# Per-feature sums of K taken from the diagonals of a row of sums, by VectorE in three separate steps

## The chip, the cores and the metric

The kernel runs on one core of a Trainium2 chip, as one launch. The metric is the device time of that launch in microseconds (us). Before the change the median of three runs is 722.59 us, the lowest 722.54 us and the highest 722.98 us. The profile is of one further execution, which took 722.83 us.

A core has five engines that run their own instruction lists and wait for each other by semaphores: TensorE (PE in the profile; its weight loads are shown apart as PEld), VectorE (DVE), ScalarE (ACT), GpSimd (POOL) and SyncE (SP), which issues the DMAs. Matrix products land in PSUM, eight banks of 128 partitions by 2 KB; all else lies in SBUF.

## The reference, cut to what matters

The layer is a residual of two branches on a layer-normalised input of 2 batches x 1024 tokens x 512 features: linear attention with 16 heads of 32 features, and a feed-forward part with low-rank experts. The change touches only the attention's sums of K.

```python
Q = jax.nn.elu(Q) + 1.0
K = jax.nn.elu(K) + 1.0
KV = jnp.einsum('bhsd,bhse->bhde', K, V)
QKV = jnp.einsum('bhsd,bhde->bhse', Q, KV)
K_sum = jnp.sum(K, axis=-2)                      # one number per batch, head and feature
QK_sum = jnp.einsum('bhsd,bhd->bhs', Q, K_sum)
out = QKV / (QK_sum[..., None] + 1e-08)
```

`K_sum` is needed twice: as the stationary operand of the product that makes the denominators `QK_sum`, and, times the bias of V, as a part of `KV`.

## The kernel before, in words

All engines but SyncE follow the order in which the program is written (a manual schedule). The sixteen tiles of 128 tokens are handled in eight pairs, `m` = 0 to 7, by `k_pair` (L421). Pairs 0 to 3 are batch 0 and pairs 4 to 7 batch 1. A pair computes K for its two tiles by seven quarter-size products (a Strassen scheme; banks `ua`, `x`, `lo`), applies elu, transposes the next tiles (bank `pt`), and multiplies the finished K tiles of the pair before by the normalised x, accumulating in the four banks `pg0` to `pg3` (`accumulate`, L410). GpSimd adds up K itself in `ksum`, 128 partitions x 512 features (`add_keys`, L412). Summing `ksum` over its partitions gives `K_sum`.

Within `k_pair` there are named places, "n", "a" and "b", where a table `hooks` (L688) hangs further work. Place "a" is behind the product 6 and its addition (L470), ahead of the transposes of the next tile; place "b" is behind the additions of L480 and L481 and ahead of the token sums of the next pair (L399 to L403). Whatever is hung there stands in every engine's list at that point.

The class `Finish` ends a batch's attention sums. `copies` moves the four `pg` banks to SBUF by ScalarE. `sums` makes `pr`, the product of a 128x128 block of ones with `ksum`: every partition of `pr` holds the whole row of 512 sums. VectorE then multiplies it by the bias of V into `ksr` (L541). `chunk_sums` makes `pc`: four products, one for each block of 128 features, with that block of `ksum` as the stationary operand and one column of ones as the moving one (L527), which puts the sums along the partitions, one column per block. VectorE copies them by four instructions into `ksd` (L531) and GpSimd shifts a second copy of it (L534). `ksd` is not read before the product `pd` of the denominators (L879, at 169 us). `values` makes `pv` and adds `ksr` to it in `kvd` (L557); `outputs` multiplies `kvd` by the output weights into the four `pko` (L562), which ScalarE copies (L563).

For batch 0 these steps hang in pairs 4 to 7: `sums` and `chunk_sums` together in pair 5, place "a". For batch 1 they hang in the first query unit (`query_unit`, L759; places named "P6", "P5" and so on after the product that they follow), which computes Q by seven products and elu with the work split over TensorE, ScalarE and VectorE.

PSUM banks are given by `Finish.bank` (L511). For batch 0 `pr0` takes bank `pt`, and `pc0` bank `x`. For batch 1 each new tile takes the next of `pg0` to `pg3` in turn, so that a tile waits for the readers of the one four places before it. After the first query unit the eight banks are handed to a new pool, whose first tiles are the five `psa` (L569), then `pxa` (L857) and `pd`.

Of the kernel before, what the change touches and what calls it, by code (L numbers as in the profile page):

```python
# [10 lines left out]
F32 = mybir.dt.float32  # L11
AF = mybir.ActivationFunctionType
ALU = mybir.AluOpType
AX = mybir.AxisListType

P = 128
# [21 lines left out]
def layer_kernel(  # L38
# [23 lines left out]
    nc = tc.nc  # L62
# [13 lines left out]
    DK = D // N_HEADS  # L76
    HPC = P // DK
    NC = D // P
# [23 lines left out]
    def pool(stack, name, bufs=1, **k):  # L102
        return stack.enter_context(tc.tile_pool(name=name, bufs=bufs, reuse_waits="tile", **k))
# [28 lines left out]
    p2w = pool(p2_stack, "p2w", bufs=2)  # L132
# [3 lines left out]
    p1 = pool(p1_stack, "p1", side="right")  # L136
    p1w = pool(p1_stack, "p1w", bufs=2, side="right")

    ident = const.tile([P, P], F32, name="ident")
# [40 lines left out]
    bv_sb = p1.tile([P, NC], F32, name="bv_sb")  # L180
# [11 lines left out]
    ones = p1.tile([P, P], F32, name="ones")  # L192
# [50 lines left out]
    def bank(name, shape=None, tag=None):  # L243
        tag = tag or (next(tags) if tags else "ps")
        return ps_pool[0].tile(shape or [P, TB], F32, tag=tag, name=name)


    warm = bank("warm", [P, NC, P], "pt")

    def warm_up(n):  # L250
# [3 lines left out]
    warm_up(WARM[0])  # L254

    pbk = bank("pbk", tag="x")
    nc.tensor.matmul(pbk, ones, bk_sb, start=True, stop=True)
    warm_up(WARM[1])
# [52 lines left out]
    def transpose_x(n, tag="pt"):  # L311
        i = TILES[n]
        pt = [bank(f"pt{i}", [P, NC, P], tag)] * 2
        if n == 0:
            pt[1] = bank("pt0_1", [P, NC, P], "ua")
        for c in range(NC):
            nc.tensor.transpose(pt[c // 2][:, c, :], xns[n][:, ts(c, P)], ident)
        for k in range(2):
            nc.scalar.copy(xnT[i // TPBATCH][k][:, :, ts(i % TPBATCH, P)], pt[k][:, 2 * k : 2 * k + 2, :])
# [101 lines left out]
    def k_pair(m, late, hooks={}):  # L421
# [69 lines left out]
        sums = pair_token_steps(2) if m == 1 else iter(())  # L491
        ea = elu_min(ka, f"ek{na}")
        next(sums, None)
        nc.vector.tensor_add(kb[:, HI], ua[:, 0:HD], bk_sb[:, HI])
        nc.vector.tensor_copy(lb, ua[:, HD:])
        elu_k(ka, ea)
        list(sums)
        eb = elu_min(kb, f"ek{nb}")
        if more:
# [4 lines left out]
    class Finish:  # L504
# [5 lines left out]

        def bank(self, name, shape=None):  # L511
            if self.b == 0:
                return bank(name, shape, "pt" if name in ("pr0", "pko0_3") else "x")

            self.made += 1
            return ps_kv_pool.tile(shape or [P, TB], F32, tag=f"pg{(self.made - 1) % NC}", name=name)

        def copies(self):
            self.gt = slot(7, [NC, D], f"gt{self.b}")
            for m in range(NC):  # L520
                nc.scalar.copy(self.gt[:, m, :], self.pg[m])

        def chunk_sums(self):

            pc = self.bank(f"pc{self.b}", [P, NC])
            for c in range(NC):
                nc.tensor.matmul(pc[:, c : c + 1], self.ksum[:, ts(c, P)], ones[:, 0:1], start=True, stop=True)  # L527
            k = ksd[self.b]
            for h in range(HPC):
                rows = slice(h * DK, (h + 1) * DK)  # L530
                nc.vector.tensor_copy(  # L531
                    k[rows, 0, :, 8 * h : 8 * h + 4], pc[rows, :].unsqueeze(2).to_broadcast([DK, NC, 4])
                )
            nc.gpsimd.tensor_copy(k[:, 1, :, 4:32], k[:, 0, :, 0:28])  # L534

        def sums(self):

            pr = self.bank(f"pr{self.b}")
            nc.tensor.matmul(pr, ones, self.ksum, start=True, stop=True)
            self.ksr = p1.tile([P, NC, P], F32, tag="ksr", name=f"ksr{self.b}")  # L540
            nc.vector.tensor_mul(  # L541
                self.ksr, bv_sb.unsqueeze(2).to_broadcast([P, NC, P]), pr.rearrange("p (c n) -> p c n", n=P)
            )

        def values(self):

# [29 lines left out]
    def route(n):  # L576

        sc = p2.tile([P, TPB, E], F32, tag="sc", name=f"sc{n}")
        nc.scalar.activation(sc, lg[n], AF.Sigmoid)
        bi = p2.tile([P, TPB, E], F32, tag="bi", name=f"bi{n}")  # L580
        nc.vector.tensor_add(bi, sc, eb_sb.unsqueeze(1).to_broadcast([P, TPB, E]))

        sh = [P, TPB, E, E]
        bj = bi.unsqueeze(2).to_broadcast(sh)
        be = bi.unsqueeze(3).to_broadcast(sh)
        gt = p2w.tile(sh, F32, tag="tmp", name=f"gt{n}", bufs=3)
        nc.vector.tensor_tensor(gt, bj, be, ALU.is_gt)
        eq = p2.tile(sh, F32, tag="eq", name=f"eq{n}")
        nc.vector.tensor_tensor(eq, bj, be, ALU.is_equal)
        nc.vector.tensor_mul(eq, eq, before.unsqueeze(1).to_broadcast(sh))  # L590
        nc.vector.tensor_add(gt, gt, eq)
        rank = bi
        nc.vector.tensor_reduce(rank, gt, AX.X, ALU.add)
        ws = wts[n // 2][:, n % 2]
        nc.vector.scalar_tensor_tensor(ws, rank, TOP_K - 0.5, sc, ALU.is_lt, ALU.mult)
        sm = p2.tile([P, TPB], F32, tag="sm", name=f"sm{n}")
        nc.vector.tensor_reduce(sm, ws, AX.X, ALU.add)
        nc.vector.tensor_scalar_add(sm, sm, DIV_EPS)
        nc.vector.reciprocal(sm, sm)
        nc.vector.tensor_scalar_mul(sm, sm, SCALE)  # L600
        nc.vector.tensor_mul(ws, ws, sm.unsqueeze(2).to_broadcast([P, TPB, E]))

    def weights_across(b):

        rows = 2 * TPB * E
        pw = fin[1].bank(f"pw{b}")
        nc.tensor.transpose(pw[0:rows, 0:P], wts[b].rearrange("p n t e -> p (n t e)"), ident)
        wx = p2.tile([rows, P], F32, tag="wx", name=f"wx{b}")
        nc.scalar.copy(wx, pw[0:rows, 0:P])
        nc.sync.dma_start(out=w_dram[b].rearrange("e t p -> t e p"), in_=wx)  # L610
        for i in range(2):
            for e in range(E):
                k = i * ER + e * RANK
                nc.sync.dma_start(
                    out=wT[b][k : k + RANK, :],
                    in_=w_dram[b][e].rearrange("t p -> (t p)").partition_broadcast(RANK),
                )
# [58 lines left out]
    for n in range(2):  # L676
# [9 lines left out]
    fin = []  # L686
# [8 lines left out]
        (6, "n"): [lambda: next(wq_sums)],  # L695
        (7, "n"): [lambda: pair_token_sums(0)],
        (4, "b"): [lambda: fin.append(Finish(0, pg, ksum)), lambda: fin[0].copies()],
        (5, "a"): [lambda: fin[0].sums(), lambda: fin[0].chunk_sums()],
        (6, "a"): [lambda: fin[0].values()],
        (6, "b"): [lambda: fin[0].outputs((0,))],  # L700
        (7, "a"): [lambda: route(0), lambda: fin[0].outputs((1,))],
        (7, "b"): [lambda: fin[0].outputs((2, 3))],
    }
# [281 lines left out]
    def last_sums():  # L985
# [7 lines left out]

    query_unit(0, {
        "P2": [last_sums],
        "P6": [lambda: fin[1].chunk_sums(), lambda: fin[1].sums(), lambda: route(3)],
        "P5": [lambda: fin[1].values(), lambda: weights_across(0)],
        "P7": [lambda: next(sums1), lambda: next(sums1), lambda: weights_across(1)],
        "P3": [lambda: fin[1].outputs((0, 1, 2, 3))],
# [532 lines left out]
    def next_pair(j):  # L1532

        pf = {}


        def pe(i):
            return lambda: pf.update({i: fold_pe(j, FREE[i], (i,))})

        def adds(i):  # L1540
            return lambda: fold_adds(j, i, pf.pop(i))

        def sums(eng, *ps):
            return lambda: list(inner_weight_sums(eng, j, ps))

        last = {}

        def last_sums(n):
            def f():
                g = last.setdefault(0, inner_weight_sums(nc.vector, j, (1, 5, 6)))  # L1550
                for _ in range(n):
                    next(g, None)

            return f

        return (
            {"6c": [pe(0)], "1d": [adds(0)], "6d": [pe(1)], "7": [adds(1)]},
            {"6c": [lambda: fold_sums(j, 0)], "2c": [lambda: fold_sums(j, 1), sums(nc.gpsimd, 3)],
             "3b": [sums(nc.gpsimd, 2), last_sums(2)], "3d": [last_sums(3)]},
        )  # L1560
# [617 lines left out]
```

## Time and profile before

| | |
|---|---|
| median of 3 runs (lowest, highest) | 722.59 us (722.54, 722.98) |
| the profiled execution | 722.83 us |
| its span, first to last instruction | 721.0 us |
| busy: PE, DVE, ACT, POOL | 714.4, 578.4, 198.3, 142.6 us |
| granted TensorE clock | 1.000 |
| 76 to 88 us: PE, DVE, ACT busy | 12.00, 9.40, 4.72 of 12 us |
| 136 to 148 us: PE, DVE, ACT busy | 12.00, 6.10, 8.23 of 12 us |
| 160 to 172 us: PE, DVE, ACT busy | 12.00, 7.60, 7.45 of 12 us |

The span is what the engines' records cover; the 1.83 us between it and the execution's time lie around it. The rows by stretch are the ones in which the changed instructions stand: pair 5 runs from about 76 to 93 us, the first query unit from about 125 to 169 us. A product of two fp32 operands appears as two passes, each with its own weight load, so that the four small products of one `pc` are eight weight loads and eight matmuls in the records. In a timeline line the first number is the start, the second the length of the merged group, and a bracket tells how long the engine had been idle and what ended that. In the chain of waits the numbers are start and length of each piece, counted from the end of what released it.

### The profile page before, as it was taken

Reading aid. Unit: us, or ns where it says so; the run is one execution under the profiler, and the core shown is the slowest. Engines: PE = TensorE matmul, PEld = TensorE weight load, DVE = VectorE, ACT = ScalarE, POOL = GpSimd, SP = SyncE. Lnnn points to the kernel's source line nnn. Section 1 sums busy time; section 2 is a strip of 40 time slices with the busy share of each in tenths; the row PEclk is TensorE's granted clock in tenths of the full one; section 3 lists DMA queues with packets and bytes.
Section 4 is the critical chain, followed back from the end, with each engine's and each line's share of the span. In section 5 each row is a group of like instructions: output and inputs, shape, how many; then the busy total and the mean of one; then the engine's idle time right before and its main releaser. Section 6 shows DMA issues by size and latency. Waiting matters only on the chain.

```text
span 721.0 us, 9901 instructions
## 1 busy us (share of the span) xinstructions
PE 714.4 (99%) x3426; PEld 491.4 (68%) x3426; DVE 578.4 (80%) x1327; ACT 198.3 (28%) x438; POOL 142.6 (20%) x176
## 2 busy tenths in 40 slices
PE   8999999999999999999999999999999999999998
PEld 6666676454434566566566566566688899899897
DVE  7788767777688678778778778878988889998884
ACT  3534413453532333333333333333200000000000
POOL 4033011101001752211211311544520100000000
PEclk9999999999999999999999999999999999999999
DMA  5243001214475101211211201334662444433101
GB/s 174 103 129 112 1 0 42 57 34 134 128 204 171 30 27 35 89 48 44 89 38 51 87 32 58 117 127 136 205 193 107 128 156 126 146 120 110 59 16 45
DMA packets 61734, 66.85 MB, mean 93 GB/s; under 512 B 10866, under 2 KB 49522, under 8 KB 61428
## 3 DMA queue, kind: packets, MB, share of 16 engines
q1 hardware_dynamic: 61154, 66.20, 29.9%
q8 instruction: 27, 0.44, 0.3%
q14 instruction: 23, 0.19, 0.1%
q10 hardware_dynamic: 530, 0.02, 0.0%
HBM read 44.11 MB, written 22.09 MB: 92 GB/s over the span
## 4 chain that ended last, share of the span: by engine, by line
PE 85%; DVE 12%; ACT 2%; issue 1%; POOL 0%; DVEq 0%; POOLq 0%
PE ab L1205 16%; PE b L1265 8%; PE po L1953 7%; PE pg L410 5%; PE pqu L778 4%; PE pya L1782 4%; PE pxa L1782 4%; PE pyb L1782 3%; PE ph L1650 3%; PE x L1205 3%; PE pxb L1782 2%; PE pyc L1782 2%; PE pxa L857 2%; PE b L1260 2%; PE pqv L778 2%; PE pr L1092 2%
## 5 line engine op out<-in xcount | busy, mean ns | idle before, releaser
L1265 PE MATMUL b<-t,w 128*128 128x512 f32 x160 | 83.2, 601 | 0.1
L410 PE MATMUL pg<-kt,xn 128*128 128x512 f32 x128 | 58.7, 594 | 0.5 <-DVE kt L354 0.5
L1287 POOL TENSOR_TENSOR r<-r,r 128x512 f32<-128x512 f32 x20 | 30.1, 1524 | 85.2 <-DVE t L1287 83.0
L1205 PE MATMUL ab<-ti,wi 128*128 128x256 f32 x180 | 45.4, 379 | 0.0
L1205 PEld LDWEIGHTS ab<-ti,w 128*128 128x128 f32 x140 | 25.1, 189 | 29.5 <-DVE r L1233 8.2
L1287 DVE TENSOR_TENSOR r<-r,r 128x512 f32<-128x512 f32 x60 | 43.2, 762 | 0.0
L1205 PEld LDWEIGHTS ab<-ti,wi 128*128 128x128 f32 x180 | 34.2, 190 | 13.2 <-issue 4.8
L1205 PE MATMUL ab<-ti,w 128*128 128x256 f32 x140 | 41.2, 387 | 0.5 <-DVE r L1233 0.2
L410 PEld LDWEIGHTS pg<-kt,xn 128*128 128x128 f32 x128 | 23.1, 190 | 22.6 <-issue 20.6
L1233 DVE TENSOR_TENSOR r<-r,ab 128x256 f32<-128x256 f32 x50 | 20.9, 419 | 21.6 <-ACT r L1230 21.1
L1238 ACT COPY r<-ab 128x256 f32<-128x256 f32 x50 | 18.6, 373 | 71.1 <-PE ab L1205 71.1
L1265 PEld LDWEIGHTS b<-t,w 128*128 128x128 f32 x160 | 29.2, 190 | 10.6 <-issue 5.9
L1241 DVE TENSOR_TENSOR r<-r,ab 128x256 f32<-128x256 f32 x50 | 20.9, 419 | 16.2 <-ACT r L1238 15.9
L1215 ACT COPY r<-ab 128x256 f32<-128x256 f32 x50 | 18.7, 374 | 48.4 <-PE ab L1205 47.1
L1953 PE MATMUL po<-wd,f 128*128 128x256 f32 x140 | 30.9, 380 | 0.1
L419 POOL TENSOR_TENSOR ksum<-ksum,kt 128x512 f32<-128x512 f32 x12 | 15.8, 1318 | 71.4 <-DVE lg L456 42.4
L1226 ACT COPY r<-ab 128x256 f32<-128x256 f32 x50 | 18.6, 373 | 40.7 <-PE ab L1205 40.7
L1896 DVE TENSOR_TENSOR f<-f 128x256 f32<-128x256 f32 x84 | 29.4, 423 | 0.1
L1953 PEld LDWEIGHTS po<-wd,f 128*128 128x128 f32 x140 | 26.4, 190 | 4.4 <-issue 0.9
L1205 PE MATMUL ab<-xnT,w 128*128 128x256 f32 x100 | 29.4, 390 | 0.0
L1205 PE MATMUL ab<-xnT,wi 128*128 128x256 f32 x100 | 28.1, 379 | 0.0
L1205 PEld LDWEIGHTS ab<-xnT,w 128*128 128x128 f32 x100 | 18.1, 189 | 10.9 <-issue 4.5
(483 smaller groups left out, 1652.1 us busy)
## 6 DMA issues: line engine op xcount, KB each, us to landing
h_dram<-h SPq DMA_DIRECT2D x40, 256.0 KB
f<-h_dram SPq DMA_DIRECT2D x10, 512.0 KB
x_ring<-in_x_dram SPq DMA_DIRECT2D x16, 256.0 KB
q_dram<-qt SPq DMA_DIRECT2D x16, 256.0 KB
xr<-in_x_dram SPq DMA_DIRECT2D x16, 256.0 KB
out_dram<-xr SPq DMA_DIRECT2D x15, 256.0 KB
w<-in_w_gate_dram SPq DMA_DIRECT2D x10, 256.0 KB
w<-in_w_up_dram SPq DMA_DIRECT2D x10, 256.0 KB
```

The costliest lines, as they stand in the source:

```text
L410: nc.tensor.matmul(pg[m], xns[n][:, ts(m, P)], kt, start=(j == 0), stop=(j == TPBATCH - 1))
L778: nc.tensor.matmul(banks[c], wqs[p][:, k, ts(c, P)], tsum[b][p][:, k, :], start=(start and k == 0), stop=(k == 1), skip_group_check=True,)
L1205: nc.tensor.matmul(out, w, t, start=start, stop=True, skip_group_check=True)
L1215: nc.scalar.copy(self.r[0][:, H0], self.ua)
L1233: nc.vector.tensor_add(self.r[1][:, H1], self.r[1][:, H1], self.lo)
L1241: nc.vector.tensor_add(self.r[1][:, H0], self.r[1][:, H0], self.lo)
L1265: nc.tensor.matmul(pb[m], ws[m][:, A_OF[p], ts(k, P)], tsum[b][p][:, k, :], start=start, stop=True, skip_group_check=True)
L1287: eng.tensor_add(to[m], t[m], v[m])
L1650: nc.tensor.matmul(phs[u][g * ER : (g + 1) * ER, :], a, f[:, g, :], start=(ns[0] == 0 and n == 0), stop=(last and n == len(chunks) - 1), s ...
L1782: nc.tensor.matmul(o, lhsT, rhs, start=first, stop=True, skip_group_check=True)
L1896: op(t[:, at, :], t[:, x_, :], t[:, y, :])
L1953: nc.tensor.matmul(ps[p][:, q, :], lhsT, rhs, start=start, stop=stop, skip_group_check=True)
```

## The change

The sums along the partitions are no longer made by TensorE. `pr` holds the row of all sums in every partition, so the sum of feature 128c + p stands in partition p at column p of block c, on the diagonal of each block. VectorE multiplies `pr` by the identity, broadcast over the four blocks (`diag`), and adds up each block along its row (`kc`). The four copies into `ksd` then read `kc` in SBUF where they read `pc` in PSUM.

The work is cut in three functions. `sums` issues only the product `pr`. `read_sums` issues the two VectorE instructions that read `pr`. `chunk_sums` issues the reduction, the four copies and the GpSimd copy. For batch 0 they stand in pair 5 "a", pair 5 "b" and pair 6 "b"; for batch 1 all three stand where both stood, in "P6", now with `sums` first. `pr0` takes bank `x`; with one tile fewer, the later tiles of batch 1 each move on by one bank.

```diff
         def bank(self, name, shape=None):
             if self.b == 0:
-                return bank(name, shape, "pt" if name in ("pr0", "pko0_3") else "x")
+                return bank(name, shape, "pt" if name == "pko0_3" else "x")
...
+        def sums(self):
+
+            self.pr = self.bank(f"pr{self.b}", [P, NC, P])
+            nc.tensor.matmul(self.pr, ones, self.ksum, start=True, stop=True)
+
+        def read_sums(self):
+            self.ksr = p1.tile([P, NC, P], F32, tag="ksr", name=f"ksr{self.b}")
+            nc.vector.tensor_mul(self.ksr, bv_sb.unsqueeze(2).to_broadcast([P, NC, P]), self.pr)
+
+            sh = [P, NC, P]
+            self.diag = p2w.tile(sh, F32, tag="tmp", name=f"diag{self.b}", bufs=3)
+            nc.vector.tensor_mul(self.diag, ident.unsqueeze(1).to_broadcast(sh), self.pr)
+
         def chunk_sums(self):
-
-            pc = self.bank(f"pc{self.b}", [P, NC])
-            for c in range(NC):
-                nc.tensor.matmul(pc[:, c : c + 1], self.ksum[:, ts(c, P)], ones[:, 0:1], start=True, stop=True)
+            kc = p1w.tile([P, NC], F32, tag="kc", name=f"kc{self.b}")
+            nc.vector.tensor_reduce(kc, self.diag, AX.X, ALU.add)
             k = ksd[self.b]
             for h in range(HPC):
                 rows = slice(h * DK, (h + 1) * DK)
                 nc.vector.tensor_copy(
-                    k[rows, 0, :, 8 * h : 8 * h + 4], pc[rows, :].unsqueeze(2).to_broadcast([DK, NC, 4])
+                    k[rows, 0, :, 8 * h : 8 * h + 4], kc[rows, :].unsqueeze(2).to_broadcast([DK, NC, 4])
                 )
             nc.gpsimd.tensor_copy(k[:, 1, :, 4:32], k[:, 0, :, 0:28])
-
-        def sums(self):
-
-            pr = self.bank(f"pr{self.b}")
-            nc.tensor.matmul(pr, ones, self.ksum, start=True, stop=True)
-            self.ksr = p1.tile([P, NC, P], F32, tag="ksr", name=f"ksr{self.b}")
-            nc.vector.tensor_mul(
-                self.ksr, bv_sb.unsqueeze(2).to_broadcast([P, NC, P]), pr.rearrange("p (c n) -> p c n", n=P)
-            )
...
-        (5, "a"): [lambda: fin[0].sums(), lambda: fin[0].chunk_sums()],
+        (5, "a"): [lambda: fin[0].sums()],
+        (5, "b"): [lambda: fin[0].read_sums()],
         (6, "a"): [lambda: fin[0].values()],
-        (6, "b"): [lambda: fin[0].outputs((0,))],
+        (6, "b"): [lambda: fin[0].outputs((0,)), lambda: fin[0].chunk_sums()],
...
-        "P6": [lambda: fin[1].chunk_sums(), lambda: fin[1].sums(), lambda: route(3)],
+        "P6": [lambda: fin[1].sums(), lambda: fin[1].read_sums(), lambda: fin[1].chunk_sums(), lambda: route(3)],
```

## The prediction, on record before the changed kernel ran

> **What bounds the kernel.** I read the page first: busy shares, then the engines' shares of the chain of waits.
>
> ```profile
> PE 714.4 (99%) x3426; PEld 491.4 (68%) x3426; DVE 578.4 (80%) x1327; ACT 198.3 (28%) x438; POOL 142.6 (20%) x176
> ...
> PE 85%; DVE 12%; ACT 2%; issue 1%; POOL 0%; DVEq 0%; POOLq 0%
> ```
>
> TensorE is the bound on the whole, and no DMA stands on the chain. But TensorE's busy time is modelled, so I next read the chain of waits from 60 to 180 us, where the touched instructions are.
>
> ```profile
> 82.08 0.86 PE pr L539 x2
> 82.94 0.79 PE pc L527 x8
> 83.72 0.65 PE pt L317 x4
> ...
> 141.97 0.79 PE pc L527 x8
> 142.76 0.97 PE pr L539 x2
> 143.73 3.43 PE pqu L778 x8
> ```
>
> The products that the change removes are on the chain both times. Until 75.67 the chain there is VectorE's; from then to 250 us it is TensorE's without a break. So TensorE time removed in pair 5 or in the first query unit counts, as far as the other engines can follow. That is the question, and the timeline answers it at each place.
>
> **What is removed.** Sixteen passes of one column. In the timeline `pc` starts at 82.77 and the transposes `pt` at 83.72: 0.95 us for eight. Those transposes also wait in the program for `ksr`'s read of bank `pt`, which ends at 82.97 + 0.69 = 83.66; with `pr0` in bank `x` that wait goes too, so they start at 82.77. In the query unit `pc` starts at 141.81, `pr` at 142.62, the next product at 143.56. With `pr` at 141.81 and its usual two passes of 0.43, that product starts at 142.67: 0.89 us. Together **1.84 us** of TensorE.
>
> Here a rule speaks against the change. The Trainium skill (TensorE: Matmul & The Clock Gate, "Back-to-back issue gap") gives a matmul of 1 to 64 columns a floor of about 25 ns; sixteen would be worth 0.40 us, as an estimate from that page, and the work given to VectorE in exchange would look dear. The row says 0.86 us for the last seven weight loads and their passes, over 0.1 us each: each pass is paced by its 128-column weight load. I take the row.
>
> **What is added on VectorE**, per batch: `diag`, the same form as L541 (0.69); the reduction of 128x512, between L593 (128x256, 0.42) and the 0.69 of a 128x512 operation, so 0.69. The four copies stay at 0.72: they read SBUF now, and small SBUF operations (L275, 0.17) cost what these did in PSUM (0.17). So 1.38 us per batch is new, and for batch 0 everything is also moved: `ksr` with `diag` (1.42 with gaps) to pair 5 "b", the reduction with the copies (1.45) to pair 6 "b". No step issues a DMA, and SP's queue is not passed. On POOL the copy of L534 (0.28) goes behind the memset of `kvd` for batch 0 and delays it by 2.3 us for batch 1, where `kvd` is wanted at 152.62: nothing. POOL's first `ksum` addition of batch 1 is released by `pr` in place of `pc`, some 0.8 us sooner: nothing.
>
> **Pair 5, batch 0.** The cover is this:
>
> ```profile
> 87.48 0.42 DVE L481 TENSOR_TENSOR kt<-kt,klo 128x256 f32<-128x256 f32 x1
> ...
> 88.72 0.43 DVE L399 TENSOR_TENSOR t<-xnT,xnT 128x256 f32<-128x256 f32 x1 [0.82 <-ACT xnT L319]
> ...
> 90.32 0.41 DVE L490 TENSOR_TENSOR kt<-kt,klo 128x256 f32<-128x256 f32 x1
> ...
> 91.90 0.69 DVE L354 SCALAR_TENSOR_TENSOR kt<-kt,ek 128x512 f32<-128x512 f32 x1 [0.29 <-ACT ek L350]
> ...
> 93.15 0.41 PEld L410 LDWEIGHTS pg<-kt,xn 128*128 128x128 f32 x2
> ```
>
> L399 waits 0.82 us for ScalarE's copy of the transposed tile. That copy stands behind a chain from the statistics (L263 to L275), which VectorE begins at 82.57 and no longer at 84.51, since `ksr` and the copies are gone from "a". Its square root is then held only by its table load: from the end of the other tile's copy, 84.12, come 1.28 (load), 0.20, 1.28 (load), 0.20 and 0.65 for the copy, so with gaps the tile is there at 87.82 (88.70 before). VectorE: L480 follows TensorE, now at 86.07; L481 ends at 86.95; `ksr` and `diag` end at 88.41; L399 starts at 88.45. So VectorE is 0.27 us earlier than before, and TensorE 0.95. Behind L399 VectorE has no idle time down to L354, so that difference of 0.68 us runs into TensorE's waits, which had these margins: product 7 of pair 6 waits for L490 (ended 90.73, load at 91.40); product 1 for L495 (91.61, 92.27); the accumulation for L354 (92.59, 93.15). All were 0.56 to 0.67. The last falls short by 0.12, and by some 0.15 with the semaphore; part may hide in the usual lead of a load over its pass. I charge **0.15**. If the statistics did not come earlier, the charge would be about 0.9. Bank `x` is a new wait: product 2 of pair 6 (its load at 89.56 after the shift, the whole TensorE list behind it) waits for `diag`, which ends at 88.41. That is covered by 1.1 us. First gain: 0.80.
>
> In pair 6 the reduction and copies go between L481 (ends 104.56 after a shift of 0.80) and L399, whose data were there at 105.6. L403 then ends at about 107.8, L490 comes 0.25 late against the shifted TensorE, and the product behind it has 0.9 us to spare (L490 ended 108.78, load at 109.72). Nothing. In pair 7 L490 again stood idle 2.77 us for TensorE: the lag is gone there.
>
> **The first query unit, batch 1.** VectorE's added 1.38 us fall before this wait, in which L581 had been idle 3.40 us since `ksr`:
>
> ```profile
> 147.59 0.23 ACT L579 ACTIVATE sc<-lg 128x32 f32<-128x32 f32 x1
> ...
> 147.85 0.19 DVE L581 TENSOR_TENSOR bi<-sc,eb_sb 128x32 f32<-128x32 f32 x1 [3.40 <-ACT sc L579]
> ...
> 159.24 0.24 ACT L609 COPY wx<-pw 64x128 f32<-64x128 f32 x1
> ...
> 159.81 0.19 PEld L562 LDWEIGHTS pko<-wo_sb,kvd 128*128 128x128 f32 x1 [0.24 <-issue]
> ...
> 164.72 0.69 DVE L837 TENSOR_TENSOR qt<-qt,pqv 128x512 f32<-128x512 f32 x1 [0.35 <-PE pqv L778]
> ```
>
> So they are hidden. But the same wait shows that ScalarE and VectorE do not move with TensorE here. ScalarE's list from the last copy of product 6 (142.01) to the sigmoid at 147.59 depends on nothing that the change advances; from 147.85 VectorE works through without idling to 155.9, then both alternate to ScalarE's copies of `pko` (162.95 to 165.00). All this stays in place while TensorE runs 0.89 us ahead, until it needs them (times here without the 0.80 of pair 5, which shifts all alike):
> - `pko3` takes the bank of `pw1` and waits for L609, which ends at 159.48. Its load stood at 159.81, would stand at 158.92, and goes at 159.54; its pass then starts 0.19 later at 159.73, against 160.23 before. 0.50 is left.
> - `psa0` now inherits the bank of `pko1`, not `pko0`: it waits for the second L563 copy, 162.95 + 2 x 0.513 = 163.98, and starts at about 164.23 against 164.52: 0.29 left.
> - `psa4` waits for the second L837, which waited 0.35 for TensorE; it can come forward only to the end of the first, 163.69 + 0.68 plus a gap: 0.31 left.
>
> From there L787, the elu and `pd` (which had about 0.3 to spare behind the last L790) follow with the same 0.31. Second gain: **0.30** of 0.89.
>
> The skill's Trace Analysis page (Perfetto Trace Analysis, "Identifying the Most-Contended Engine") would name the engine of highest occupancy and have it relieved first; by that all 1.84 us count, and TensorE is indeed busy 12.00 of 12 us from 160 to 172. The three waits above say 1.10. I go by the waits.
>
> **Sum.** 0.80 + 0.30 = 1.10 us. Later the chain alternates between TensorE and VectorE with no DMA on it, so I let the gain pass whole to the end. The profiled execution, 722.83 us (721.0 span, 1.83 around it), gives 721.7; it stands 0.24 above the median of the runs, from which the same gain gives 721.5. I say **721.6 us**.
>
> **The rivals.**
> 1. *Both gains in full* (721.0, 24%). For it: both `pc` groups are on the chain, and the margins at `pko3` and `psa` are near 0.3, of the size of my reading errors in lead times. Against it: three separate waits would have to be softer than they look.
> 2. *VectorE is short in pair 5* (722.3, 14%). The statistics do not come earlier, or `diag` and its neighbour cost more: TensorE waits about 0.9 at L354, and only 0.35 us of gain is left in all.
> 3. *VectorE's added and moved work is not hidden at all* (slower, 10%). Its place is behind L481 in pairs 5 and 6 and in "P6"; its price is 1.42 + 1.45 + 1.38 = 4.25 us against 1.84 saved: +2.4, 725.0. It decides once more than 1.84 of those 4.25 reach TensorE. Against it: the idle times of 0.82 and 3.40 us stand just there.
> 4. The change not doing what it says: TensorE's list has eight small products fewer, so only their price could be wrong. At the skill's floor of 25 ns 0.40 us would be all: a small gain or none, inside case 2.
>
> **How the numbers follow.** The forecast has 52%. A measurement of this kernel can tell about 0.2%, 1.45 us, from no change. Case 1 is faster by more than that for the most part, and so are some of the forecast's larger values: 0.30. Case 3 gives slower, mostly: 0.09. The rest, 0.61, is within. The bounds of the gain are 1.84 above, and nothing or a little loss below (both second-site waits worse, pair 5 short): 720.8 to 723.0 leaves out most of case 3 and little else.
>
> **What would show it.** Right: `pt` starts right behind `pr`; L399 of pair 5 has no ScalarE wait and the accumulation of pair 6 shows a short wait for L354; the sigmoid-to-`pko` stretch keeps its length from product 6 while `pko3` and `psa` show waits for ScalarE. Wrong: `psa` 1.7 us earlier than before (case 1), a wait of half a us or more at L490 or L354 (cases 2, 3), or a gain in the query unit that is lost or grown behind 240 us.

## The result, and the profile after

| | before | after |
|---|---|---|
| median (lowest, highest; runs) | 722.71 us (721.91, 723.52; 17) | 721.15 us (720.51, 721.71; 17) |
| the profiled execution | 722.83 us | 720.87 us |
| its span | 721.0 us | 719.1 us |

The ratio is 0.9978, with a 95% interval of 0.9972 to 0.9985: 1.56 us faster (1.1 to 2.0), where the sum of the prediction was 1.10. The median lies 0.45 us below the predicted 721.6. The head of the page and the engines' shares of the chain of waits, after:

```profile
span 719.1 us, 9872 instructions
...
PE 712.2 (99%) x3410; PEld 488.9 (68%) x3410; DVE 581.7 (81%) x1331; ACT 198.2 (28%) x438; POOL 143.0 (20%) x176
...
PE 84%; DVE 13%; ACT 2%; issue 1%; POOL 0%; DVEq 0%; POOLq 0%
```

TensorE has 16 passes and 16 weight loads fewer, VectorE four instructions and 3.3 us more. The page says no more than that; where the time went is read from the chain of waits, whose columns are start, length, engine, tile and line:

```profile
81.33 0.86 PE pr L526 x2
82.19 0.44 PE pt L317 x4
82.62 1.72 PE pg L410 x4
...
140.22 0.86 PE pr L526 x2
141.08 3.43 PE pqu L781 x8
144.52 3.57 PE pv L554 x32
...
155.18 2.58 PE pko L564 x6
157.78 1.12 PE pko L564 x2
158.90 3.43 PE pqv L781 x8
162.34 1.43 PE psa L571 x10
163.76 3.44 PE pxa L860 x8
```

The same places in before, as far as the prediction does not show them:

```profile
75.67 1.13 PE klo L439 x4
...
157.82 3.43 PE pko L562 x8
...
164.69 1.27 PE psa L569 x10
165.96 3.44 PE pxa L857 x8
```

Starts of two executions can't be subtracted as they stand. This one is already 0.76 us ahead at the product 7 of pair 5 (74.91 against 75.67 us), before anything that the change touches, and nearly all of it arose in the first 13 us. I therefore count from that product and call what is left TensorE's **lead** over before. It is 0.99 us at the `pg` products behind `pr`, and 1.88 at the product behind the second `pr`. Then it shrinks at two places: to 1.59 between the `pko` of 155.18 and that of 157.78 (in before one unbroken piece of eight), and to 1.44 at `pxa` behind `psa`. It stays at 1.43 to 1.45 up to 500 us; there about 0.29 is lost, and at the end of the span 1.17 is left. So of the 1.9 us by which the two spans differ, 0.76 is none of the change's doing, and the lead of 1.44 fits the runs' 1.56.

Pair 5 and the start of pair 6 in the timeline after:

```profile
85.73 0.42 DVE L481 TENSOR_TENSOR kt<-kt,klo 128x256 f32<-128x256 f32 x1
86.07 0.68 DVE L530 TENSOR_TENSOR ksr<-bv_sb,pr 128x512 f32<-128x512 f32 x1
...
86.67 0.68 DVE L534 TENSOR_TENSOR diag<-ident,pr 128x512 f32<-128x512 f32 x1
...
87.26 0.42 DVE L399 TENSOR_TENSOR t<-xnT,xnT 128x256 f32<-128x256 f32 x1
...
88.85 0.41 DVE L490 TENSOR_TENSOR kt<-kt,klo 128x256 f32<-128x256 f32 x1
...
89.65 0.84 PEld L439 LDWEIGHTS klo<-wk_sums,t 128*128 128x128 f32 x4
...
90.48 0.69 DVE L354 SCALAR_TENSOR_TENSOR kt<-kt,ek 128x512 f32<-128x512 f32 x1 [0.35 <-ACT ek L350]
...
91.40 0.41 PEld L410 LDWEIGHTS pg<-kt,xn 128*128 128x128 f32 x2
```

L399 no longer waits for ScalarE, as predicted. But look at the starts of `ksr`, `diag` and L399: they are 0.60 and 0.59 us apart, though each record is 0.68 long. Queued behind each other, two such instructions cost 1.19 us, and L399 stands at 87.26, which is 88.02 in before's count; the prediction had 88.45. The profile of before had this price already. In its first query unit two additions of the same size take 1.28 us together with records of 0.68, so that the second starts 0.60 behind the first:

```profile
138.82 1.28 DVE L807 TENSOR_TENSOR qt<-qt,pqx 128x512 f32<-128x512 f32 x2
```

In pair 5 after, L354 ends at 91.17, 0.23 ahead of the load at 91.40, and L490 at 89.26, 0.39 ahead of its load. There is no stall.

The first query unit in the timeline after:

```profile
145.84 0.23 ACT L581 ACTIVATE sc<-lg 128x32 f32<-128x32 f32 x1
...
146.10 0.19 DVE L583 TENSOR_TENSOR bi<-sc,eb_sb 128x32 f32<-128x32 f32 x1 [2.23 <-ACT sc L581]
...
157.48 0.24 ACT L611 COPY wx<-pw 64x128 f32<-64x128 f32 x1
...
157.78 0.30 PEld L564 LDWEIGHTS pko<-wo_sb,kvd 128*128 128x128 f32 x2 [0.85 <-ACT wx L611]
...
162.31 1.26 PEld L571 LDWEIGHTS psa<-ident,sa 128*128 128x128 f32 x10 [0.81 <-ACT gt L565]
```

VectorE waits for the sigmoid for 2.23 us, where it waited 3.40: the added instructions fell into that wait. The two brackets on PEld are the new waits: `pko3` for the copy of `pw1`, `psa` for the second copy of `pko`. A third wait is hidden inside the group of ten loads of `psa`. Taken load by load, the trace has the ninth, the first of `psa4`, at 163.27, which is 0.18 us behind the eighth where 0.11 is the usual distance, and 0.05 behind the end of VectorE's second L840 (L837 before) at 163.22. It is the last of the three, so it sets the lead of 1.44 at `pxa`.

### The profile page after: what moved, and what is told of

Same layout as the page of the kernel before. It is cut to its first block, busy times and chain, and to the rows that moved or that the text cites. A ratio compares the mean times of both kernels' runs of the same rounds, so it can differ in the third digit from the quotient of the medians.

```text
span 719.1 us, 9872 instructions
## 1 busy us (share of the span) xinstructions
PE 712.2 (99%) x3410; PEld 488.9 (68%) x3410; DVE 581.7 (81%) x1331; ACT 198.2 (28%) x438; POOL 143.0 (20%) x176
## 4 chain that ended last, share of the span: by engine, by line
PE 84%; DVE 13%; ACT 2%; issue 1%; POOL 0%; DVEq 0%; POOLq 0%
PE ab L1208 16%; PE b L1268 8%; PE po L1956 7%; PE pg L410 5%; PE pqu L781 4%; PE pya L1785 4%; PE pxa L1785 4%; PE pyb L1785 3%; PE ph L1653 3%; PE x L1208 3%; PE pxb L1785 2%; PE pyc L1785 2%; PE pxa L860 2%; PE b L1263 2%; PE pqv L781 2%; PE pr L1095 2%
```

## The experiments

Leads are TensorE's leads over before as above, at three points: behind pair 7 (about 124 us), at the first `pxa` (about 165 us), and at the end. For one source and one execution to the next, the first two repeat within 0.02 us. Medians are set beside before's in the same group: 722.71 us for the first four experiments, 722.62 for the next four, 722.61 for the last three.

**Batch 0 alone.** Batch 1 keeps its four products: `chunk_products` makes them and their copies into `ksd`, `read_row` makes `ksr` alone. In this and the following edits only the lines that matter are shown.

```diff
-        "P6": [lambda: fin[1].sums(), lambda: fin[1].read_sums(), lambda: fin[1].chunk_sums(), lambda: route(3)],
+        "P6": [lambda: fin[1].chunk_products(), lambda: fin[1].sums(), lambda: fin[1].read_row(), lambda: route(3)],
```

> Batch 0 by diagonals as in the changed kernel, batch 1 by the four products as before. Measured in the chain of waits as TensorE's lead over before, counted from product 7 of pair 5 (klo at 75.67 us in before, so that jitter of the first loads is left out): my theory says 1.0 us at the pg accumulation of pair 5 and unchanged 1.0 at pxa; time about 1.0 us under before (ratio 0.9986). Rival 'VectorE short in pair 5': a lead of 0.4 or less. Rival 'the gain is jitter of the start': no lead.

Median 721.76 us, ratio 0.9984 (0.9978 to 0.9991), leads 0.99, 1.00 and 1.03. The first gain arrives in full and goes through the query unit undiminished: what pair 5 gains moves ScalarE and VectorE too, and only what TensorE gains on them within the query unit meets the waits there.

**Batch 1 alone.** Batch 0 keeps its products in pair 5 "a", with `pr0` in bank `pt`.

```diff
-        (5, "a"): [lambda: fin[0].sums()],
-        (5, "b"): [lambda: fin[0].read_sums()],
+        (5, "a"): [lambda: fin[0].sums(), lambda: fin[0].read_row(), lambda: fin[0].chunk_products()],
...
-        (6, "b"): [lambda: fin[0].outputs((0,)), lambda: fin[0].chunk_sums()],
+        (6, "b"): [lambda: fin[0].outputs((0,))],
```

> Batch 1 by diagonals as in the changed kernel, batch 0 by the four products as before. My theory: the lead is 0.90 us at the product behind pr, and ScalarE's copies of pw1 and pko cut it to about 0.45 at pxa; time about 0.45 us under before (ratio 0.9994). Rival 'both gains in full': 0.9 at pxa too. Rival 'all lost to ScalarE': 0 at pxa.

Median 722.07 us, ratio 0.9995 (0.9987 to 1.0003), which by itself is not told from no change. The leads tell it: 0.89 behind `pr`, 0.60 at `psa`, 0.45 at `pxa`, 0.48 at the end. The two halves add up: 1.00 + 0.45 = 1.45 against 1.44 for the whole.

**The sigmoid earlier, in the changed kernel and in before.** The sigmoid of the last routing step is taken right behind those of steps 1 and 2, so that ScalarE does not go back to it between two exponentials. `scores` holds the sigmoid's lines, which stood in `route`; the new call stands behind the routes 1 and 2.

```diff
-        sc = p2.tile([P, TPB, E], F32, tag="sc", name=f"sc{n}")
-        nc.scalar.activation(sc, lg[n], AF.Sigmoid)
+        sc = early.get(n) or scores(n, "sc")
...
+        early[3] = scores(3, "sc3")
```

> The changed kernel, with the sigmoid of route(3) taken next to those of route(1) and route(2), before the first copies of pg; the rest of route(3) stays. This takes two table loads and the sigmoid out of ScalarE's list in the first query unit, on which route(3) and all behind it hung. My theory (ScalarE's sigmoid anchors the unit and cuts batch 1's gain): pko3 and psa wait for ScalarE no more and the lead at pxa is 1.9 us, 0.45 more than the changed kernel's 1.45; time about 0.45 under the changed kernel, 2.0 under before (ratio 0.9973). Rival (the loss sits in bank order or in VectorE's added work, not in the sigmoid): lead 1.45, time that of the changed kernel.

> The kernel before with the same early sigmoid. My theory: TensorE did not wait for ScalarE in this unit, so there is nothing to win but the 0.1 to 0.2 us that psa waits; lead 0 to 0.2 us at pxa, time within 0.2 us of before. Rival (the early sigmoid is a gain by itself): 0.45 us or more here as well.

The changed kernel comes to 720.51 us, ratio 0.9974 (0.9964 to 0.9983), with leads of 0.99, 1.89 and 1.90. Its chain of waits:

```profile
156.96 3.43 PE pko L564 x8
160.39 3.43 PE pqv L787 x8
163.82 1.27 PE psa L571 x10
165.09 3.44 PE pxa L866 x8
```

The eight `pko` are one piece again and `psa` has its old length of 1.27: nothing waits any longer than in before. Two table loads of 1.28 us are gone from ScalarE's list in this stretch (from 138 to 172 us the trace has one, not three), and with them all the waits that capped the lead; I call such a wait a **cap**. The Trainium skill (ScalarE: Activation LUTs, "Rules for kernel authors") advises grouping functions by table set; here, at `pxa`, that is worth 0.45 us of TensorE's time, but only beside the change. In before the same edit gives 722.61 us, ratio 1.0 (0.9991 to 1.0008), with leads of 0, 0 and 0.02: there TensorE set the time, and ScalarE's 2.56 us bought nothing. 1.89 us is thus what the sixteen passes cost TensorE, 0.12 us each.

**Everything in pair 5 "a"**, the first place of the old work:

```diff
-        (5, "a"): [lambda: fin[0].sums()],
-        (5, "b"): [lambda: fin[0].read_sums()],
+        (5, "a"): [lambda: fin[0].sums(), lambda: fin[0].read_sums(), lambda: fin[0].chunk_sums()],
...
-        (6, "b"): [lambda: fin[0].outputs((0,)), lambda: fin[0].chunk_sums()],
+        (6, "b"): [lambda: fin[0].outputs((0,))],
```

> All three steps of batch 0 in pair 5 'a', where the kernel before had them; the rest as changed. Lead of TensorE over before, counted from product 7 of pair 5, in the chain of waits. My theory (the split places the work beside idle time of VectorE): diag, reduction and copies now stand ahead of the statistics, ScalarE's copy of the next tile comes about 1.8 us later than in the changed kernel, L354 and product 4 make TensorE wait 1.0 to 1.5 us, and the lead behind pair 6 is -0.5 to 0 instead of 0.99; time about 1.2 us above the changed kernel. Rival (places do not matter, removing the products is all): lead 0.99.

Median 722.76 us, ratio 1.0005 (0.9997 to 1.0013); leads −0.67, −0.21, −0.17. The chain of waits leaves TensorE at `pr` and comes back only with a product of pair 6:

```profile
81.70 0.87 PE pr L526 x2
82.60 0.69 DVE ksr L530
83.28 0.61 DVE diag L534
83.92 0.70 DVE kc L538
...
85.37 0.71 DVE st L263
...
87.53 1.28 ACT L280
...
89.59 0.42 DVE t L399
...
91.27 0.34 DVE kt L490
91.65 1.13 PE klo L439 x4
```

In front of the statistics (`st`) VectorE's whole new work delays ScalarE's square root, the tile behind it, and all of pair 6: 1.66 us lost against the changed kernel. That is a little more than the range I expected. The third rival's mechanism is at work here, at a price of 1.66 us where it had put 2.87 on pair 5 and 6. The query unit then brings 0.46, about what it brings the changed kernel (0.99 to 1.44): a delay of pair 5 moves ScalarE and VectorE too, so the caps stand, with waits of 0.85 us at `pko3` and 0.80 at `psa`.

**The reduction and copies in pair 5 "b"**, with `ksr` and `diag`:

```diff
-        (5, "b"): [lambda: fin[0].read_sums()],
+        (5, "b"): [lambda: fin[0].read_sums(), lambda: fin[0].chunk_sums()],
...
-        (6, "b"): [lambda: fin[0].outputs((0,)), lambda: fin[0].chunk_sums()],
+        (6, "b"): [lambda: fin[0].outputs((0,))],
```

> Reduction and copies of batch 0 directly behind diag in pair 5 'b' instead of pair 6 'b'; the rest as changed. My theory: VectorE's run from L399 to L354 comes 1.4 us later, its margin before the pg accumulation in the changed kernel is 0.23 us, so TensorE waits about 1.1 and the lead behind pair 6 is about -0.2; time about 1.1 us above the changed kernel. Rival (places do not matter): lead 0.99.

Median 722.82 us, ratio 1.0002 (0.9994 to 1.001); leads −0.37, 0.09, 0.11. The chain of waits:

```profile
87.47 0.61 DVE diag L534
...
88.10 0.70 DVE kc L538
...
91.31 0.34 DVE kt L490
...
91.70 1.13 PE klo L439 x4
```

The statistics are early here, and yet 1.36 us is lost against the changed kernel, where I expected about 1.1. The reduction and copies take 1.45 us, and L490 stands 1.65 later than in the changed kernel, against a margin of 0.39. So 1.27 is lost by the start of the `pg` products, and 0.09 at the accumulation behind L354. For batch 0, splitting the work over pairs 5 and 6 is what makes the change pay.

**`diag` made twice in pair 5 "b"**: one more instruction of the disputed kind in the disputed place.

```diff
-        (5, "b"): [lambda: fin[0].read_sums()],
+        (5, "b"): [lambda: fin[0].read_sums(), lambda: fin[0].again(1)],
```

> The changed kernel with diag of batch 0 made twice in pair 5 'b' (0.60 us more of VectorE). My theory: margin 0.23 us at L354 and 0.2 of a weight load's lead, so 0.2 to 0.4 us of it reach TensorE: lead behind pair 6 0.6 to 0.8. Rival (VectorE has room there): 0.99. Rival (none is hidden): 0.39.

Median 721.68 us, ratio 0.9989 (0.9982 to 0.9995); leads 0.56, 1.02, 1.08. Of the added instruction 0.43 us reaches TensorE, just more than the 0.2 to 0.4 that I expected. The timeline:

```profile
87.96 0.69 DVE L538 TENSOR_TENSOR diag<-ident,pr 128x512 f32<-128x512 f32 x1
...
90.16 0.41 DVE L490 TENSOR_TENSOR kt<-kt,klo 128x256 f32<-128x256 f32 x1
...
90.62 0.73 PEld L439 LDWEIGHTS klo<-wk_sums,t 128*128 128x128 f32 x4 [0.43 <-DVE kt L490]
...
91.79 0.69 DVE L354 SCALAR_TENSOR_TENSOR kt<-kt,ek 128x512 f32<-128x512 f32 x1 [0.35 <-ACT ek L350]
```

The bracket on PEld puts the wait at L490, where I had expected it at L354. By the start of the `pg` products 0.33 us is lost, and only the last 0.1 falls to the accumulation that waits for L354. This second `diag` writes the same tile as the first and starts 0.71 us behind it, not 0.60. What it shows is how near the edge pair 5 stands: the cover has a few tenths of a microsecond left.

**The reduction repeated**: twice in pair 6 "b", four times in "P6".

```diff
-            nc.vector.tensor_reduce(kc, self.diag, AX.X, ALU.add)
+            for _ in range(4 if self.b else 2):
+                nc.vector.tensor_reduce(kc, self.diag, AX.X, ALU.add)
```

> The changed kernel with the reduction made twice for batch 0 (pair 6 'b') and four times for batch 1 ('P6'): 0.64 and 1.9 us more of VectorE, in idle times read as 0.75 and 2.23 us in the changed kernel. My theory: all hidden, lead at pxa 1.44 as in the changed kernel, time the same within 0.2 us. Rival (VectorE's work has a price wherever it stands): 2.5 us more, or a good part of it.

Median 721.39 us, ratio 0.9985 (0.9978 to 0.9991). Leads of 1.00 and 1.33: one more reduction in pair 6 costs nothing; three more in the query unit cost 0.11 us, where I expected nothing. The timeline shows why anything is lost at all:

```profile
143.46 2.85 DVE L539 TENSOR_REDUCE kc<-diag 128x4 f32<-128x512 f32 x4
...
146.86 0.23 ACT L582 ACTIVATE sc<-lg 128x32 f32<-128x32 f32 x1
...
147.12 0.31 DVE L584 TENSOR_TENSOR bi<-sc,eb_sb 128x32 f32<-128x32 f32 x1
```

The four take 2.85 us, 0.71 apiece. The three added ones are 2.14 us, the wait for the sigmoid was 2.23, and its bracket is gone: the spare time is used up, and L584 takes 0.31 us where it took 0.19, about the 0.11 lost. This also refutes the third rival for the changed kernel. The end lead of this one execution was −0.37: 1.7 us of it was lost between 492 and 505 us. The median of 21 runs shows no such loss.

**The copy of `pw1` by VectorE**, ahead of the token sums, to take `pko3`'s wait away by itself:

```diff
-        nc.scalar.copy(wx, pw[0:rows, 0:P])
+        (nc.vector.tensor_copy if b else nc.scalar.copy)(wx, pw[0:rows, 0:P])
...
-        "P7": [lambda: next(sums1), lambda: next(sums1), lambda: weights_across(1)],
+        "P7": [lambda: weights_across(1), lambda: next(sums1), lambda: next(sums1)],
```

> The changed kernel with the copy of pw1 (L611) made by VectorE ahead of the token sums of batch 1, where the changed kernel's ScalarE makes it at 157.48 us. That takes away the wait of pko3 alone; psa still waits for ScalarE's copies of pko. My theory (two caps in series, both hung on the same sigmoid): the lead over before is 1.88 at pko and product 4, and falls back to 1.25 to 1.45 at pxa, since VectorE's list got 0.2 us longer; time that of the changed kernel or up to 0.2 above. Rival (the wait of pko3 is the loss): 1.75 or more at pxa, time 0.3 us less.

Median 721.19 us, ratio 0.9981 (0.9974 to 0.9987); lead at `pxa` 1.44, as without the edit. `pko` no longer waits, and the timeline has the time one place later:

```profile
163.63 1.26 PEld L571 LDWEIGHTS psa<-ident,sa 128*128 128x128 f32 x10 [1.09 <-ACT gt L565]
```

The wait for the copies of `pko` was 0.81 us and is 1.09, and the ninth load waits for L840 as before (0.18 us behind the eighth). The caps stand in series, so the narrowest, which is the last, decides.

**The changed kernel and its early sigmoid once more.**

> The changed kernel once more, beside the other two on one chip. Lead 1.44 at pxa in the chain of waits whatever the start; ratio to before 0.9978 to 0.9984.

> The changed kernel with the early sigmoid once more, beside it. My theory: lead 1.89 at pxa, 0.45 us under the changed kernel of this call; ratio to before about 0.9973. Rival (its gain in the first call was chance): the time of the changed kernel.

The changed kernel: 721.28 us, ratio 0.9982 (0.9973 to 0.9991), leads 0.99, 1.44, 1.49. With the early sigmoid: 720.74 us, ratio 0.9973 (0.9962 to 0.9984), leads 1.00, 1.89, 1.94. The intervals of the two ratios overlap, and the gap rests on few executions; but in this group five of the seven with the early sigmoid lie below nine of the ten without, and both pairs of medians (0.64 and 0.54 us apart) agree in direction with the 0.45 us that the traces show at `pxa`. The early sigmoid on top of the change is the best version that was run.

## Why the prediction was right, and where it was off

- **What is removed**: 0.95 + 0.89 = 1.84 us predicted, 1.89 measured with nothing in the way. The row of before was the right price. The floor of about 25 ns for a short matmul (the Trainium skill, TensorE: Matmul & The Clock Gate, "Back-to-back issue gap") would have left 0.40 us for all sixteen, as an estimate from that page; the measured 0.12 us each is almost five times that. But the same section gives this floor for a matmul by itself, and says of a stream of weight loads and matmuls that both set the spacing, so it did not speak against the change as the prediction has it. The traces agree: the 32 passes of `pv`, 128 columns wide with a weight load each, take 3.57 us, 0.11 each, so that a pass of one column came no cheaper than one of 128.
- **Pair 5**: this is the term that was mis-sized. The step "`ksr` and `diag` end at 88.41; L399 starts at 88.45" took 1.46 us for the two, from the length of one record plus gaps. They cost 1.19, as the pairs in before's profile would have told. (The rest of the 0.43 us by which L399 came earlier: `ksr` too starts before the record in front of it ends, and TensorE was a little further ahead.) The 0.15 charged at L354 became a margin of 0.23, the short wait that was to show there did not appear, and the first gain was 0.99 in place of 0.80. VectorE is not without idle time from L399 to L354, as the prediction says: the line that it shows has 0.29 us there for ScalarE's L350; but L350 follows L349 and moves along with it. The rest of the step held: the statistics came early, L399's wait for ScalarE is gone, and bank `x` caused no wait.
- **Pair 6**: no cost, as predicted. The doubled reduction shows that there was room for another.
- **The query unit**: the mechanism held at each point. ScalarE's list did not move, `pko3` kept 0.60 of 0.89 (predicted 0.50), and `psa` and `pxa` 0.45 (predicted 0.30). At `pko3` the prediction let the pass start 0.19 us behind its load, the length of the load's record; product 4 starts 0.96 behind that load (158.74 against 157.78), which is two passes of 0.43 and only 0.10. At `psa` the prediction had two waits of nearly one size, 0.29 and 0.31. The trace tells them apart: the wait of `psa4` for L840 ends last, and without it some 0.07 us more would be left. For that wait the prediction put the second L837 behind the whole record of the first; they start 0.60 apart (161.94 and 162.54 after), and with 0.60 the 0.31 would have been 0.43. So the query unit was mis-sized by the same error as pair 5. That all these caps hang on ScalarE's list with the late sigmoid, with which VectorE alternates, is shown by the run that shortens it.
- **The sum**: 1.10 predicted, 1.44 by the lead at `pxa`: 0.19 of the difference from pair 5, 0.15 from the query unit. Whether all of it reaches the end differs between single executions: 1.17 in this one, 1.49 in the second.
- **The rule on the busiest engine** would have counted 1.84. TensorE was indeed busy without a break, and 0.44 us of the removed work still turned into waits for ScalarE and VectorE. The section that the prediction names (the Trainium skill, Perfetto Trace Analysis, "Identifying the Most-Contended Engine") also makes an exception of TensorE, which the prediction leaves out: its headroom is not judged by the busy share of matmuls but, among others, by that of the weight loads, here 68%.
- **The rivals**: both gains in full is not the changed kernel's case (1.44 at `pxa`, not 1.88), but it is what the early sigmoid makes of it. The time alone would not have told the two apart: 721.15 us is nearer to this rival's 721.0 than to 721.6. VectorE short in pair 5 did not happen, though one extra instruction brings it about. Work not hidden at all is refuted at the places that the change uses; at two others 1.36 and 1.66 us were lost, so that most of the work showed there, but not all.
- **The bound of 0.2%**: the gain of 1.56 us came out just past the 1.45 that the chances were drawn at, where 0.61 had been put on a smaller change. The two corrections above brought it close to that bound; on which side it fell is chance, as the lead of 1.44 lies just below it and the interval of 1.1 to 2.0 us on both sides.

## What to carry to other kernels

Work taken from the busiest engine is worth what the engines beside it let through: follow the freed time forward to the first thing that the engine takes from another engine's fixed list, and look for the next such cap behind the first. A stretch of queued instructions is priced by the distance of their starts in the trace, not by the sum of their records, above all where a margin of 0.2 us decides; the profile before the change may already hold such pairs. And where a step stands matters more than its size: split over two places with time to spare, the same instructions gained TensorE 0.99 us; put together in one place, they lost it 0.37 or 0.67.

## What the runs showed of the hardware that was not expected

- Two 128x512 multiplications of VectorE that do not depend on each other start 0.60 us apart with records of 0.68. A reduction of the same size behind `diag`, which it reads, starts 0.70 to 0.71 behind, and so do repeated writes of one tile. The Trainium skill (VectorE: DVE Perf Modes, "The DRAIN you can't avoid") says that the next operation waits until the pipe is empty, and that one which is not held starts earlier. The independent pairs agree with the latter, by 0.08 us per instruction; what holds the others was not tried.
- From product 7 of pair 5 to 250 us TensorE's chain repeats within 0.02 us in the two kernels that were profiled twice, while the times of one kernel spread over more than 1 us. Where the traces put the spread: the start (that product stands at 74.91 to 76.69 us in the thirteen profiles) and a stretch near 498 us, where GpSimd's additions of `wd` run beside VectorE's work. There a pair of VectorE operations took 2.11 us in the profile after and 1.82 in before, and leads changed by 0 to 1.7 us between executions. Why it differs from one execution to the next was not tried.
